# Attention's projection pieces in halves over two steps, with a new order of GpSimd's queue, in a fused attention and feed-forward kernel

## The chip, the cores and the metric

The kernel runs on one core of a Trainium2 chip. A core has TensorE (matmuls, which read SBUF and write PSUM), VectorE (called DVE in the profile), ScalarE (ACT), GpSimd (POOL), and DMA queues that SyncE (SP) issues. Each engine works through its own instructions in order and waits on semaphores for the others. The metric is the device time of one execution in microseconds (us); lower is better. Before the change it is 2101.75 us, the median of 3 runs (2101.75 to 2103.98).

## The reference

Two sandwiched layers over x of 8 batches, each 512 rows by 512 columns, in float32:

```python
x = x + _layernorm(_L0_attn_ref(_layernorm(x, axis=-1), ...), axis=-1)
x = x + _layernorm(_L0_ffn_ref(_layernorm(x, axis=-1), ...), axis=-1)
```

Attention has 16 heads of 32 columns. The head is all rotary (32 of 32), so key and query are the rotated ones:

```python
c_kv = x @ W_dkv + b_dkv                       # 512 -> 128
v = (c_kv @ W_uv + b_uv)                       # 128 -> 512
c_q = x @ W_dq + b_dq                          # 512 -> 128
q_rot = _apply_rotary(c_q @ W_qr + b_qr)       # 128 -> 512
k_rot = _apply_rotary(x @ W_kr + b_kr)         # 512 -> 512
attn = softmax(q @ k.T / sqrt(32))             # per head
out = (attn @ v) @ W_o + b_o
```

`_apply_rotary(t)` is t * cos + swap(t) * sin, where swap exchanges the halves of each head. The feed-forward part transforms its input by a Walsh-Hadamard matrix, multiplies with W_up and W_gate (512 -> 2048), takes silu(gate) * up, transforms again and multiplies with W_down. Both transforms are orthogonal and linear, and the kernel applies the second one to W_down instead of the activations; it calls this folding.

## The kernel before

Attention runs first, all eight batches one after the other, then the feed-forward part, which the change does not touch. In the profiled execution attention's steps run from about 48 us to 894 us, after a start-up in which batch 0's first projections are made.

**Steps.** The scores of a batch are worked out as 4 groups of 4 heads (`NK`), and a group as 4 blocks of 128 keys (`NT`), so a batch is 16 steps and attention 128. Step i of batch b is written b.i here; its place in the group is c = i mod 4, and n counts the groups. The loop `for t in range(NG * NT)` issues one step, and every engine's queue is the order in which this loop writes its instructions: the region is scheduled by hand.

TensorE gets these groups of matmuls in each step, in this order:

1. `scores_t`: the transposed scores t of this key block, for four heads in two PSUM buffers of two banks each. Bfloat16 rows with minus the row maximum come first (the bias rows, L564), then key times query (L573). ACT takes the exponential of each half into p (L585).
2. `weigh`: the previous step's p times the values, into one bank for the whole group (ops, L606).
3. In c = 3, `bias_rows` (L550): the next group's row maxima are transposed into rows. In c = 2, `sums` (L623): the softmax denominators of the group before.
4. `row_max`: the untransposed scores s of the step that comes `AHEAD` = 6 steps later (L527). DVE takes the maximum over each row (L535, two instructions a step). `split` cuts the maxima of a whole group into three bfloat16 parts on GpSimd (L543 to L545); it is issued in c = 1.
5. A piece: a part of the next batch's projections, of the previous batch's output projection, or of the folding.

**Pieces.** They are `key` (L439, four matmuls of 512 columns), `query` (L454, one), `value` (L466, one), `compress` (L407, four, for `ckv` and `cq`), `out_proj` (L661 and L662), `x_flip` (L394, transposes of the normalized x), and `fold` (L485, one matmul; after it four levels of additions on DVE, L493 and L494, one a step, kept in the list `levels`). Which piece stands in which step is in the tables `BETWEEN` (put before s) and `BEHIND` (put last), with `FIRST_` versions for batch 0; the steps in `TWO` have their `BETWEEN` piece just ahead of the `BEHIND` one. A piece "behind" writes the single PSUM bank of `ps_f`, which the sums and the transposed bias rows use too. Where a step has two pieces, the first is wide (here called "beside") and takes a buffer of `ps_s`, the ring of three two-bank buffers in which s and t live (`bank`, L388).

**Rotations.** `rotate` lets ACT copy a key or query piece from PSUM to SBUF (`lin`) and puts the rest, a closure, in the list `turns`: a shuffle on DVE (L420) and three GpSimd operations (L421 to L423). `turn` empties that list; it is called twice a step, once directly behind the exponentials and once behind the row maxima. So a piece of one step is rotated at the start of the next.

**Other work on DVE, GpSimd and ACT.** In c = 1 and 3 GpSimd adds the p of neighbouring key blocks (`add_up`, L594, four operations of 128x512); in c = 0 of the next group DVE adds the two sums (`add_pairs`, L599). DVE also inverts and divides (L644, L657) and makes the statistics of the normalizations (L99, L100); GpSimd works out the inverse standard deviations (L104, L105) and adds the residual (L694). ACT copies the pieces out of PSUM and normalizes x (`x_norm`). `load_x`, `x_stats`, `x_shift`, `x_norm` and `x_flip` bring in the x of two batches later; `early` and `later` set their steps. `fold_load` reads a slice of W_down for a fold, at the steps in `READ`; the folds stand at the steps in `FOLDS`.

In the last batch there is no next batch to project. There, `in_step` puts the first feed-forward inputs through their transposes and Hadamard matmuls (L195, L207), at the places in `ENTRY`, and the last keys, queries and values of batch 7 (key 3, query 3, values 2 and 3) stand in its steps 0 to 3, as in every batch.

Of the kernel before, what the change touches and what calls it, by code (L numbers as in the profile page):

```python
# [10 lines left out]
F32 = mybir.dt.float32  # L11
# [22 lines left out]
def sandwich_kernel(  # L34
# [207 lines left out]
    with ExitStack() as actx:  # L242
# [25 lines left out]
        def load_row(b, t):  # L268

            if b < NB - 1:  # L270
                xr[b, t] = row.tile([P, D], F32, tag="xr", name=f"xr_{b}_{t}", bufs=2)
            else:
                xr[b, t] = fo.tile(
                    [P, D], F32, tag="wwza"[t], name=f"xr_{b}_{t}", bufs=2 - t // 2
                )
            nc.sync.dma_start(out=xr[b, t], in_=x[b, ts(t, P), :])
# [137 lines left out]
        def rotate(dst, ps, bias, scale, name, first=None, second=None):  # L414
            lin = rp.tile([P, S], F32, tag="lin", name=f"lin_{name}")
            nc.scalar.activation(lin, ps, AF.Identity, bias=bias, scale=scale)

            def rest():
                rot = rp.tile([P, S], F32, tag="rot", name=f"rot_{name}", bufs=2)
                nc.vector.stream_shuffle(rot, lin, swap)  # L420
                (first or nc.gpsimd).tensor_mul(lin, lin, cs[:, 0, :])  # L421
                (second or nc.gpsimd).tensor_mul(rot, rot, cs[:, 1, :])
                (first or nc.gpsimd).tensor_add(dst, lin, rot)  # L423

            turns.append(rest)
# [3 lines left out]
        def turn():  # L429

            while turns:
                turns.pop(0)()

# [48 lines left out]
        def fold(n, wide=False):  # L482
            _, w = folds.pop(0)
            ps = bank(wide, f"fd_{n}").rearrange("p (c m) -> p c m", c=NI)
            nc.tensor.matmul(ps, lhsT=h128, rhs=w, start=True, stop=True)  # L485
            z = fo.tile([P, NI, NF], F32, tag="z", name=f"fz_{n}")
            a = fo.tile([P, NI, NF], F32, tag="a", name=f"fa_{n}")
            nc.scalar.copy(z, ps)
# [22 lines left out]
        levels = []  # L511

# [247 lines left out]
        for t in range(3):  # L760
# [13 lines left out]
        BETWEEN = {  # L774
            0: (x_flip, 1, 1), 1: (x_flip, 1, 2), 4: (x_flip, 1, 3),
            8: (query, 1, 0), 9: (query, 1, 1), 12: (query, 1, 2), 13: (x_flip, 2, 0),
        }
        BEHIND = {
            0: (value, 0, 2), 1: (key, 0, 3), 2: (query, 0, 3), 3: (value, 0, 3),
            5: (compress, 1, "cq"), 6: (key, 1, 0), 7: (out_proj, -1, 0),  # L780
            8: (out_proj, -1, 1), 9: (out_proj, -1, 2), 10: (out_proj, -1, 3),
            11: (key, 1, 1), 12: (compress, 1, "ckv"), 13: (value, 1, 0), 14: (key, 1, 2),
            15: (value, 1, 1),
        }

        FIRST_BETWEEN = {i: p for i, p in BETWEEN.items() if i not in (8, 9)}
        FIRST_BEHIND = {
            **BEHIND, 7: (query, 1, 0), 8: (None, NB, None), 9: (key, 1, 1),
            10: (None, NB, None), 11: (query, 1, 1),
        }  # L790
# [5 lines left out]
        FOLDS = [4, 10, 15] + [NK * NT * b + i for b in range(1, NB - 1) for i in (4, 10)]  # L796
        FOLDS.append(NK * NT * (NB - 1) + 1)
        READ = [0] + [g - 3 for g in FOLDS[1:]]


        TWO = (8, 9, 10, 12, 15)

        def piece(table, b, i, wide=False):
            if b == 0 and table is BEHIND and i == 8:
                out_bias()
            pieces = table if b else FIRST_BETWEEN if table is BETWEEN else FIRST_BEHIND
            if i in pieces:
                fn, d, what = pieces[i]
                if 0 <= b + d < NB:
                    fn(b + d, what, *([True] if wide else []))  # L810
            at = NK * NT * b + i
            if at in FOLDS and (table is BETWEEN) == (b > 0 and i in TWO or i == 15 or b == NB - 1):
                fold(FOLDS.index(at), wide)
            if b == NB - 1 and (i, table is BEHIND) in ENTRY:
                in_step(*ENTRY[i, table is BEHIND], 2 * NT)
# [18 lines left out]
        def early(b, i):  # L834

            if b > 0 and i - 3 in OUT:
                residual(b - 1, OUT[i - 3])
            if b + 2 < NB and i in (12, 14, 15):
                x_norm(b + 2, max(i - 13, 0))
            if i == 0 and 0 < b + 1 < NB:  # L840
                x_norm(b + 1, 3)

        def later(b, i):
# [7 lines left out]
            if b + 2 < NB:  # L851
                if i == 4:
                    load_x(b + 2, NT)
                elif 6 <= i < 10:
                    x_stats(b + 2, i - 6)
                elif i == 11:
                    x_shift(b + 2)

        for t in range(NG * NT):
# [8 lines left out]
            turn()  # L868
# [5 lines left out]
            if last_steps:  # L874
                piece(BETWEEN, b, i)
# [12 lines left out]
            if not last_steps and (i not in TWO or b == NB - 1):  # L888
                piece(BETWEEN, b, i)
# [8 lines left out]
            turn()  # L898
# [5 lines left out]
            if levels and (c > 0 or 0 < i and b < 1):  # L904
                levels.pop(0)()
            if small:
# [20 lines left out]
            if i in TWO and b < NB - 1:  # L927
                piece(BETWEEN, b, i, True)
            piece(BEHIND, b, i)
# [685 lines left out]
```

## Time and profile before

| | before |
|---|---|
| median of 3 runs | 2101.75 us |
| the profiled execution's own time | 2102.66 us |
| its span, first to last instruction | 2100.9 us |
| granted TensorE clock, mean | 0.999 |
| TensorE busy with matmuls | 2076.8 us, 99% of the span, 9035 instructions |
| TensorE weight loads | 1057.4 us, 50% |
| GpSimd | 1575.4 us, 75% |
| DVE | 1414.4 us, 67% |
| ACT | 745.3 us, 35% |
| DMA | 218.12 MB, 104 GB/s over the span |

The profile is one execution, so sums are made against its 2102.66 us and not against the median. A matmul counts as busy from when TensorE takes it up until its modelled end, which includes time in which it waits inside the engine; a busy share of 99% therefore does not say that no time is lost. A row of the timeline has the start in us, the duration, the engine, the line of the kernel, and the operation with its output and inputs and their shapes; "x4" means that the row stands for four instructions. A remark in square brackets is the wait ahead of it and what ended it.

### The profile page before, as it was taken

To read this page: it belongs to the slowest core of one execution; us is meant where nothing else is said; L and a number is where in the kernel's file an instruction comes from. 1 tells how busy PE (TensorE), PEld (TensorE's weight loads), DVE (VectorE), ACT (ScalarE), POOL (GpSimd) and SP (SyncE) were. 2 spreads that over 40 slices of the span, in tenths; PEclk is the share of its full clock that TensorE was granted. 3 is DMA by queue.
4 is the path that set the end of the run, shared out by engine and by line. 5 is a ranking of instruction groups with operands and counts; after the bars stand their busy time and mean duration, and the time that the engine had idled before them with its cause. 6 is when DMAs were issued, how large, how long until landed. Compare 5 with 4: busy or idle time off the path is not lost.

```text
span 2100.9 us, 26741 instructions
## 1 busy us (share of the span) xinstructions
PE 2076.8 (99%) x9035; PEld 1057.4 (50%) x9042; DVE 1414.4 (67%) x2356; ACT 745.3 (35%) x1199; POOL 1575.4 (75%) x1629
## 2 busy tenths in 40 slices
PE   8999999999999999999999999999999999999998
PEld 4333333333333333344444677676676766777753
DVE  5698777676767677465545866678866678656542
ACT  3554545555555545522121122222222222222211
POOL 4787979787878889645453678788888879787852
PEclk9999999999999999999999999999999999999999
DMA  3112121212121122237454444444343344444432
GB/s 122 37 31 51 42 54 49 47 51 52 46 57 46 32 66 72 70 104 221 145 166 152 146 143 148 133 138 149 130 157 131 131 137 144 138 158 136 138 112 70
DMA packets 215913, 218.12 MB, mean 104 GB/s; under 512 B 87376, under 2 KB 147920, under 8 KB 215776
## 3 DMA queue, kind: packets, MB, share of 16 engines
q1 hardware_dynamic: 215424, 215.32, 33.2%
q8 instruction: 72, 1.18, 0.2%
q0 software_dynamic: 352, 1.08, 0.1%
q14 instruction: 65, 0.53, 0.1%
HBM read 169.18 MB, written 46.92 MB: 103 GB/s over the span
## 4 chain that ended last, share of the span: by engine, by line
PE 94%; DVE 3%; issue 1%; POOL 1%; ACT 1%; DMA 0%; SPq 0%; POOLq 0%; DVEq 0%; ACTq 0%
PE d L1123 24%; PE psy L1225 18%; PE s L527 6%; PE ops L606 6%; PE ps_k L439 5%; PE ps_y L662 5%; PE t L573 5%; PE u L1106 5%; PE g L1106 4%; PE psz L1516 3%; PE t L564 3%; PE l L623 2%; PE ps_q L454 2%; PE ps_v L466 1%; PE ps_cq L407 1%; PE fxh L207 1%
## 5 line engine op out<-in xcount | busy, mean ns | idle before, releaser
L1225 PE MATMUL psy<-wd,g 128*128 128x512 f32 x896 | 448.9, 592 | 0.0
L535 DVE TENSOR_REDUCE nm<-s 128x2 f32<-128x1024 f32 x256 | 300.8, 1216 | 175.1 <-PE s L527 175.1
L1347 POOL TENSOR_TENSOR pr<-pr,pr 128x512 f32<-128x512 f32 x294 | 391.6, 1357 | 9.0
L594 POOL TENSOR_TENSOR p<-p,p 128x512 f32<-128x512 f32 x244 | 330.2, 1384 | 22.1 <-PE ops L606 22.1
L585 ACT ACTIVATE p<-t 128x1024 f32<-128x1024 f32 x256 | 251.8, 1023 | 89.0 <-PE t L573 89.0
L1123 PE MATMUL d<-xb,wq 128*128 128x256 f32 x992 | 254.2, 380 | 1.9 <-DVE inner L1139 1.4
L1123 PEld LDWEIGHTS d<-tt,wq 128*128 128x128 f32 x864 | 164.0, 190 | 144.4 <-issue 106.0
L1123 PE MATMUL d<-tt,wq 128*128 128x256 f32 x864 | 233.8, 379 | 0.2 <-DVE pr L1144 0.2
L1140 POOL TENSOR_TENSOR pr<-inner 128x256 f32<-128x256 f32 x168 | 126.0, 750 | 138.5 <-DVE inner L1139 105.9
L1123 PEld LDWEIGHTS d<-xb,wq 128*128 128x128 f32 x992 | 186.7, 190 | 62.4 <-issue 30.1
L1225 PEld LDWEIGHTS psy<-wd,g 128*128 128x128 f32 x896 | 169.7, 190 | 49.3 <-issue 29.4
L1136 ACT COPY inner<-d 128x256 f32<-128x256 f32 x168 | 62.6, 373 | 309.6 <-PE d L1123 291.5
L1132 ACT COPY inner<-d 128x256 f32<-128x256 f32 x168 | 62.6, 372 | 300.3 <-PE d L1123 193.2
L527 PE MATMUL s<-kT,qT 32*128 32x512 f32 x1024 | 153.8, 639 | 0.7 <-DVE nm L535 0.7
L573 PE MATMUL t<-qT,kT 32*128 32x512 f32 x1024 | 142.8, 598 | 0.0
L606 PE MATMUL ops<-p,v 128*32 128x512 f32 x1024 | 136.8, 605 | 0.0
L1142 POOL TENSOR_TENSOR pr<-pr,inner 128x256 f32<-128x256 f32 x168 | 136.5, 813 | 0.0
L1123 PE MATMUL d<-T,wq 128*128 128x256 f32 x496 | 127.6, 380 | 0.2
L1144 DVE TENSOR_TENSOR pr<-d,inner 128x256 f32<-128x256 f32 x168 | 70.5, 420 | 75.5 <-PE d L1123 72.9
L439 PE MATMUL ps_k<-xT,wkr_sb 128*128 128x512 f32 x256 | 118.3, 605 | 0.7 <-ACT xT L397 0.7
L662 PE MATMUL ps_y<-wo_sb,oT 128*128 128x512 f32 x256 | 115.8, 593 | 0.9 <-DVE oT L657 0.6
L1135 DVE TENSOR_TENSOR inner<-d,inner 128x256 f32<-128x256 f32 x168 | 70.5, 419 | 62.4 <-PE d L1123 62.0
(219 smaller groups left out, 3263.8 us busy)
## 6 DMA issues: line engine op xcount, KB each, us to landing
wq<-wdeep SPq DMA_DIRECT2D x168, 448.0 KB, 4.2
wd<-wdd SPq DMA_DIRECT2D x112, 256.0 KB, 2.8
wdeep<-w SPq DMA_DIRECT2D x32, 448.0 KB, 5.5
xr<-in_x SPq DMA_DIRECT2D x32, 256.0 KB, 2.8
xin<-x1d SPq DMA_DIRECT2D x32, 256.0 KB, 4.0
xres<-x1d SPq DMA_DIRECT2D x32, 256.0 KB, 3.3
out<-fy SPq DMA_DIRECT2D x32, 256.0 KB, 2.0
rec<-rd SPq DMA_DIRECT2D x124, 64.0 KB, 2.0
```

The lines of the kernel that those rows point to most:

```text
L439: nc.tensor.matmul(ps, lhsT=wkr_sb[:, k, ts(g, P)], rhs=xT[b][:, k, :], start=(k == 0), stop=(k == NK - 1),)
L527: nc.tensor.matmul(sp[j // 2][:, j % 2, :], lhsT=qT[b][rows, g, ts(qc, P)], rhs=kT[b][rows, g, :], start=True, stop=True,)
L535: nc.vector.tensor_reduce(nms[n][:, qc, 2 * h : 2 * h + 2], sp[h], AX.X, ALU.max, negate=True)
L573: nc.tensor.matmul(sp[j // 2][:, j % 2, :], lhsT=kT[b][rows, g, ts(c, P)], rhs=qT[b][rows, g, :], start=False, stop=True,)
L585: nc.scalar.activation(pt[n, c, h], sp[h], AF.Exp)
L594: nc.gpsimd.tensor_add(into, into, pt[n, c, j // 2][:, j % 2, :])
L606: nc.tensor.matmul(o_ps[n][j * DH : (j + 1) * DH, :], lhsT=vv[b][:, c, ds(g * P + j * DH, DH)], rhs=pt[n, c, j // 2][:, j % 2, :], start=( ...
L662: nc.tensor.matmul(ps, lhsT=oT[b][:, k, ts(qc, P)], rhs=wo_sb[:, k, :], start=False, stop=(k == NK - 1),)
L1106: nc.tensor.matmul(ps, lhsT=w[:, SLOT[n], k, :], rhs=rhs[:, k, :], start=k == 0, stop=k == 1)
L1123: nc.tensor.matmul(ps, lhsT=w[:, INNER[m]], rhs=rhs[m], start=True, stop=True)
L1225: nc.tensor.matmul(ys_[t], lhsT=g[:, ts(t, P)], rhs=w, start=n == 0, stop=n == NI - 1)
L1347: nc.gpsimd.tensor_add(pr[n][:, h], pr[a][:, h], pr[b][:, h])
```

## The change

It touches attention's steps alone.

**Pieces in halves.** `both(b, i, small, large)` puts a small piece (a query, a value or a fold) together with a large one (a key or a compress) over steps i and i + 1. Each step makes half the columns of both (256 of 512), the small piece in one half of the `ps_f` bank and the large one in the other half, and two ACT copies take them out. There are 40 such pairs; a step of a pair has all its matmuls of these pieces at 256 columns. The tables are replaced by `put`, which writes a dictionary `plan` from step and place ("between", "beside", "behind") to work.

**A new layout of the batch.** In batches 1 to 6 pairs stand at steps 1, 3, 5, 11, 13 and 15 (the last reaching into the next step 0); the four values stand beside the output projections in steps 7 to 10; x is flipped between, in steps 9, 12, 13 and the next step 0, for two batches later. Key 3 and query 3 are made with the others in the batch before. In batch 6 the pair at 13 is taken apart: key 3 of batch 7 is made in 6.14, and query 3 in 7.2, while values 2 and 3 of batch 7 are made in batch 6. Two folds stand in batch 7, at 7.3 and at 7.8. Batch 6's step 15 and batch 7's steps 0 and 1 have no piece behind; of the first feed-forward input, step 7.0 has the transposes, as before.

**Rotations.** `turn(True)` runs one rotation at a time. The first place, ahead of `weigh`, is used in c = 0 and 2 and in step 13 alone; the second, behind the row maxima, in c = 0, 1 and 3 except in step 13. In c = 1 and 3 GpSimd's block sums, and in c = 1 the split too, so come before the rotation in its queue; in step 13 the rotation still comes first.

**Rest.** x is loaded at step 14 of three batches earlier, its statistics made at steps 1, 2, 3 and 5, its shift at step 7 and its norms at 8, 11, 12 and 14 (all moved). Fold levels run in c = 0 in batch 7 alone (before: in batch 0 alone), and one of the small operations of `small` (batch 0's output bias) waits while a level runs. The last batch's residual rows use the fold's buffers in another order.

The core of the diff:

```diff
             lin = rp.tile([P, S], F32, tag="lin", name=f"lin_{name}")
             nc.scalar.activation(lin, ps, AF.Identity, bias=bias, scale=scale)
+            rotation(dst, lin, name, first, second)
+        def rotation(dst, lin, name, first=None, second=None):
...
             while turns:
                 turns.pop(0)()
+                if one:
+                    return
         def key(b, g, wide=False):
             if g == 0:
...
+            n, w = folds.pop(0)
             ps = bank(wide, f"fd_{n}").rearrange("p (c m) -> p c m", c=NI)
             nc.tensor.matmul(ps, lhsT=h128, rhs=w, start=True, stop=True)
             z = fo.tile([P, NI, NF], F32, tag="z", name=f"fz_{n}")
+            nc.scalar.copy(z, ps)
+            fold_levels(n, w, z)
+        def fold_levels(n, w, z):
             a = fo.tile([P, NI, NF], F32, tag="a", name=f"fa_{n}")
...
             def level(src, dst, h):
                 sv = src.rearrange("p (a t b) n -> p a t (b n)", t=2, b=h)
...
             )
         levels = []
...
+        HC = S // 2
+        split_in_two = {}
+        def half(h, ps, fn, b, what):
+            cols = ts(h, HC)
...
+                if h == 0:
+                    split_in_two["z"] = fo.tile([P, NI, NF], F32, tag="z", name=f"fz_{n}")
+                z = split_in_two["z"]
+                blocks = ts(h, NI // 2)
+                pv_ = ps.rearrange("p (c m) -> p c m", m=NF)
+                nc.tensor.matmul(pv_, lhsT=h128, rhs=w[:, blocks, :], start=True, stop=True)
+                def leave():
+                    nc.scalar.copy(z[:, blocks, :], pv_)
+                    if h == 1:
+                        folds.pop(0)
+                        fold_levels(n, w, z)
+                return leave
+            if fn is value:
+                if what == h == 0:
...
+                if what == h == 0:
+                    qT[b] = qkv.tile([P, NK, S], F32, tag="qT", name=f"qT_{b}")
+                if h == 0:
+                    split_in_two["q"] = rp.tile([P, S], F32, tag="lin", name=f"lin_q{b}_{what}")
+                dst = split_in_two["q"]
+                nc.tensor.matmul(
+                    ps, lhsT=wqr_sb[:, ts(what, P)], rhs=cT[b, "cq"][:, cols], start=True, stop=True
+                )
+                def leave():
+                    nc.scalar.activation(
+                        dst[:, cols], ps, AF.Identity, bias=bqs[:, what : what + 1], scale=QSCALE
+                    )
+                    if h == 1:
+                        rotation(qT[b][:, what, :], dst, f"q{b}_{what}")
...
-        BETWEEN = {
-            0: (x_flip, 1, 1), 1: (x_flip, 1, 2), 4: (x_flip, 1, 3),
-            8: (query, 1, 0), 9: (query, 1, 1), 12: (query, 1, 2), 13: (x_flip, 2, 0),
-        }
-        BEHIND = {
-            0: (value, 0, 2), 1: (key, 0, 3), 2: (query, 0, 3), 3: (value, 0, 3),
-            5: (compress, 1, "cq"), 6: (key, 1, 0), 7: (out_proj, -1, 0),
-            8: (out_proj, -1, 1), 9: (out_proj, -1, 2), 10: (out_proj, -1, 3),
-            11: (key, 1, 1), 12: (compress, 1, "ckv"), 13: (value, 1, 0), 14: (key, 1, 2),
-            15: (value, 1, 1),
-        }
...
+        plan = {}
+        def put(b, i, place, *work):
+            if len(work) == 1 or work[1] < NB:
+                plan.setdefault((NK * NT * b + i, place), []).append(work)
+        def both(b, i, small_, large):
+            large = large if large[1] < NB else None
+            small_ = small_ if len(small_) == 1 or small_[1] < NB else None
+            if large and small_:
+                for h in range(2):
+                    put(b, i + h, "behind", halves, 0, h, small_, large)
+            elif small_:
+                put(b, i, "behind", *small_)
+        def halves(_, h, small_, large):
+            ps = bank(False, f"ps_{large[0].__name__}_{large[1]}_{large[2]}_{h}")
+            both_ = [(*small_, None, None)[:3], large]
+            for leave in [half(h, ps[:, ts(n, HC)], *which) for n, which in enumerate(both_)]:
+                leave()
+        both(0, 0, (value, 0, 2), (key, 0, 3))
+        put(0, 2, "behind", query, 0, 3)
+        put(0, 3, "behind", value, 0, 3)
+        both(0, 4, (fold,), (compress, 1, "cq"))
+        both(0, 6, (query, 1, 0), (key, 1, 0))
+        put(0, 8, "behind", out_bias)
+        both(0, 9, (query, 1, 1), (key, 1, 1))
+        put(0, 11, "beside", query, 1, 2)
+        put(0, 11, "behind", compress, 1, "ckv")
+        both(0, 12, (value, 1, 0), (key, 1, 2))
+        put(0, 14, "beside", query, 1, 3)
+        put(0, 14, "behind", key, 1, 3)
+        for t in range(3):
+            put(0, 15 + t, "beside", value, 1, t + 1)
+        both(0, 15, (fold,), (compress, 2, "cq"))
+        for t, i in enumerate((0, 1, 4)):
+            put(0, i, "between", x_flip, 1, t + 1)
+        for b in range(NB):
+            for t, i in enumerate((9, 12, 13, 16)):
+                put(b, i, "between", x_flip, b + 2, t)
+        for b in range(1, NB):
+            both(b, 1, (query, b + 1, 0), (key, b + 1, 0))
+            both(b, 3, (query, b + 1, 1), (compress, b + 1, "ckv"))
+            if b < NB - 1:
+                both(b, 5, (fold,), (key, b + 1, 1))
+            for t in range(NT):
+                put(b, 7 + t, "beside", value, b + 1, t)
+                put(b, 7 + t, "behind", out_proj, b - 1, t)
+            both(b, 11, (query, b + 1, 2), (key, b + 1, 2))
+            if b == NB - 2:
+                put(b, 13, "behind", fold)
+                put(b, 14, "behind", key, NB - 1, 3)
+                put(b, 18, "behind", query, NB - 1, 3)
+                continue
+            both(b, 13, (query, b + 1, 3), (key, b + 1, 3))
+            if b < NB - 1:
+                both(b, 15, (fold,), (compress, b + 2, "cq"))
+        put(NB - 1, 3, "behind", fold)
+        put(NB - 1, 8, "beside", fold)
...
+        READ = [1]
+        for b in range(NB - 1):
+            READ += [NK * NT * b + 10 + 2 * (b < NB - 2), NK * NT * (b + 1) + 2]
+        READ[-1] = NK * NT * (NB - 1)
+        READ.append(NK * NT * (NB - 1) + 4)
+        def piece(place, b, i):
+            for fn, *which in plan.get((NK * NT * b + i, place), ()):
+                fn(*which, *([True] if place == "beside" else []))
+            entry = i, {"between": False, "behind": True}.get(place)
+            if b == NB - 1 and entry in ENTRY:
+                in_step(*ENTRY[entry], 2 * NT)
...
-            if b + 2 < NB and i in (12, 14, 15):
-                x_norm(b + 2, max(i - 13, 0))
-            if i == 0 and 0 < b + 1 < NB:
-                x_norm(b + 1, 3)
+            if b + 2 < NB and i in NORMS:
+                x_norm(b + 2, NORMS.index(i))
+            if b == i == 0:
+                x_norm(1, 3)
...
             ends_group = c == NT - 1 and n + 1 < NG
             if not ends_group:
                 second()
-            turn()
+            if c in (0, 2) or i == 13:
+                turn(True)
             if c == 0 and n > 1:
...
-            if not last_steps and (i not in TWO or b == NB - 1):
-                piece(BETWEEN, b, i)
+            if not last_steps:
+                piece("between", b, i)
...
                 if u % NT == NT - 1:
                     split(u // NT)
             early(b, i)
-            turn()
+            if c != 2 and i != 13:
...
-            if levels and (c > 0 or 0 < i and b < 1):
+            busy_dve = False
+            if levels and (c > 0 or b == NB - 1):
+                busy_dve = len(levels) % 5 != 1
                 levels.pop(0)()
-            if small:
+            if small and not busy_dve:
                 small.pop(0)()
             if t in READ:
                 fold_load(READ.index(t))
...
-            if i in TWO and b < NB - 1:
-                piece(BETWEEN, b, i, True)
-            piece(BEHIND, b, i)
+            piece("beside", b, i)
+            piece("behind", b, i)
```

## The prediction

> **What bounds the kernel now.** I read the page's slices, then its chain of waits, then TensorE's timeline through attention. [...]
>
> ```profile
> PE   8999999999999999999999999999999999999998
> ...
> POOL 4787979787878889645453678788888879787852
> ...
> PE 94%; DVE 3%; issue 1%; POOL 1%; ACT 1%; DMA 0%; SPq 0%; POOLq 0%; DVEq 0%; ACTq 0%
> ```
>
> TensorE is busy in every slice and is 94% of the chain, so time can come only from gaps between its instructions. They hide in stretched rows; I take the distance from one group's start to the next one's. Attention's 128 steps run from 48 to 894 us; two of them:
>
> ```profile
> 270.52 0.40 PE L564 MATMUL t<-brow,ones_b 32*128 32x512 bf16 x4
> 270.74 1.03 PE L573 MATMUL t<-qT,kT 32*128 32x512 f32 x8
> 271.70 1.07 PE L606 MATMUL ops<-p,v 128*32 128x512 f32 x8
> ...
> 273.56 1.14 PE L527 MATMUL s<-kT,qT 32*128 32x512 f32 x8
> 274.63 1.13 PE L454 MATMUL ps_q<-cq,wqr_sb 128*128 128x512 f32 x2
> 275.69 0.71 PE L564 MATMUL t<-brow,ones_b 32*128 32x512 bf16 x4
> 276.02 1.24 PE L573 MATMUL t<-qT,kT 32*128 32x512 f32 x8
> 277.19 1.06 PE L606 MATMUL ops<-p,v 128*32 128x512 f32 x8
> ```
>
> From bias to ops is 1.18 us in the first and 1.50 in the second, which follows a piece of only 1.06: there half of the bias rows wait for a PSUM buffer that DVE's first row maximum (1.2 each) still holds. So a short piece costs the next step 0.32. Adding all such excesses over each group's usual distance gives about 30 us: 7.4 in batch 0, 2.7 in each of batches 2 to 5, a little less in 1 and 6, some 7 in batch 7. That is all there is to win. The batches last 100.9, 108.6, four times 108.7, 108.1 and 93.5.
>
> **A step of the new plan.** Bias 0.23, t 0.96, ops 1.00, s 1.07: 3.26. Every fourth step adds sums (0.86), another one bias transposes (0.33); a flip is 0.59. A whole key piece is 3.63, a small one 1.06.
>
> **Halving: +1.5.** 40 pairs are cut; in each, 10 matmul records of 512 columns become 20 of 256. The FFN's timeline has both widths:
>
> ```profile
> 1303.25 1.02 PE L1225 MATMUL psy<-wd,g 128*128 128x512 f32 x2
> 1304.11 1.03 PE L1123 MATMUL d<-tt,wq 128*128 128x256 f32 x4
> 1304.97 0.59 PE L1225 MATMUL psy<-wd,g 128*128 128x512 f32 x1
> ```
>
> Four of 256 take 0.86, two of 512 take 0.86: a pair costs 20 x 0.216 - 10 x 0.428 = 0.04 more. [...] The row shows this very form, weights loaded for each record, at half; I take the row (0 to 3). The number of changes between tiled and full matmuls stays. The halves' ACT copies (0.37 each for 128x256 on the page, two 0.8, against 0.69 whole) end before the exponentials at 1.3 into the step.
>
> **Short steps filled: -10.9.** Every middle step now ends with 2.36 (halves of a pair) or more, and DVE's first maximum is out 1.3 after s. 34 waits of 0.32 in batches 1 to 6 go. What is late next is s, for an exponential: 0.2 in four steps a batch (5, 8, 9, 12; now 1, 4, 5, 8), which stays; batch 6, without flips, gets three more, **+0.6**.
>
> **Values beside out_proj: +4.8.** They move to steps 7 to 10. A "beside" piece takes the fifth buffer in a ring of three, that of the second t, so it waits for the second exponential, which comes late in a step with bias transposes. 0.15 shows it:
>
> ```profile
> 145.31 1.14 PE L527 MATMUL s<-kT,qT 32*128 32x512 f32 x8
> 146.98 1.12 PE L485 MATMUL fd<-fw,h 128*128 128x512 f32 x2 [0.53 <-ACT p L585]
> ```
>
> 0.6 each in step 7 of six batches and in 0.11 and 0.15 (4 to 5 in all). Behind it waits out_proj, hence all of TensorE.
>
> **Rotations behind the splits: +5.0.** From step 13 to the next step 1 GpSimd's queue is now: q2, block sums, split, residual, k2, sums, q3, k3, sums, split. Rotations 4 x 3.84, sums 3 x 4.9, splits 2 x 1.5, residual 1.25: 34.3, each from an undisturbed stretch of its timeline. Beside it DVE adds tensors in SBUF, and the two collide. The pair sums alone, then against GpSimd:
>
> ```profile
> 422.58 2.35 DVE L599 TENSOR_TENSOR p<-p,p 128x1024 f32<-128x1024 f32 x2
> ...
> 454.97 4.20 DVE L599 TENSOR_TENSOR p<-p,p 128x1024 f32<-128x1024 f32 x2
> ...
> 455.96 2.13 POOL L423 TENSOR_TENSOR kT<-lin_k,rot_k 128x512 f32<-128x512 f32 x1
> 458.05 2.26 POOL L694 TENSOR_TENSOR y<-xr,y 128x512 f32<-128x512 f32 x1
> ```
>
> Both lose 1.9. [...] The rows give 1.9, 0.4 and 0.2 each, 2.7, which I take. The queue starts 3.2 into step 13, behind DVE's pair sums and shuffle, and ends 40.2 after that step's start. TensorE wants the second split's rows after 6.2+6.5+5.9+6.2+5.8+6.5 = 37.1, plus 2.2 into step 3: 39.3. Late by 0.9 to 1.0, in step 3 of batches 2 to 6; s and all TensorE stand behind. Bounds: on time (0)[...]. Step 13's exception keeps q2 early: its buffer is needed by the third key's copy, which ACT would reach 0.4 before the rotation ends; ACT's exponential just misses the delay.
>
> **DVE: +1.2 (0 to 4).** With GpSimd busy from step 15 to 6, a fold level costs DVE about 2 instead of 0.8 (L494 is seen at 0.42 and 1.48), pair sums 4.2. DVE then runs up to 2 us behind, its first maximum 0.1 to 0.4 ahead of t: I take 0.2 a batch.
>
> **Batch 0: -5.4.** 6 us of work come in (two flips, key, query, half a compress, less folds) and leave batches 6 and 7; over all batches this is nil. Of 7.4 stall about 2 stay: DVE, 23.9 and 23.3 busy of 25 from 100 to 150 us, loses 1.5 folds, and the bias's small steps avoid fold levels. Bounds -3 and -6.
>
> **Batch 7: +7.5.** It loses 4.7 us of work, but 6.15, 7.0 and 7.1 are left without any piece, and t waits for DVE there. 6.15 makes 7.0's bias wait 1.3. In 7.0 DVE has shuffle, level, xflat and statistics ahead of its maxima, then pair sums and a level ahead of 7.1's. With these at their undisturbed times 7.0 to 7.2 stall 5.1; at their contended times 9.7; now it is 1.8. So 3.3 to 8; GpSimd's queue (k2, sums, k3, sums) runs through, so near the upper. A second fold in step 8 is work, counted above.
>
> **At nothing.** Norms, statistics and loads of x move within a batch: ACT is 35% busy, statistics keep their number, and SP now issues x's 1 MB load at step 14, three steps before its first use (now two), waiting there for the last norm; behind it SP has only loads due later. No TensorE wait now ends with a DMA. Fold reads stay about three steps ahead. If a load were late, DVE's statistics would hold up the maxima: a few us once a batch. FFN is untouched.
>
> **Sum.** 1.5 - 10.9 + 0.6 + 4.8 + 5.0 + 1.2 - 5.4 + 7.5 = +4.3. The profiled execution took 2102.66 (span 2100.9), so 2107.0; the median shown is 0.9 less: **2106.1**.
>
> **Rivals.**
> *Not slower:* GpSimd's queue is in time. The split at step 3 decides: if the queue ends 1.0 earlier (DVE's sums meeting its pauses), the 5.0 fall away, DVE keeps its slack (-1.2) and 7.0 to 7.2 pay 5.1 (-4): 2096. For it: 1 in 40 is within my reading. Against: there is no pause between step 13 and 2. 0.3.
> *GpSimd decides:* the split comes 2.5 late and ACT's half copy waits for a rotation: +8, so 2114. For it: nothing has slack; against: a batch has 91 us of GpSimd work in 108. 0.2.
> *The stalls stay:* the change doesn't even out the steps, DVE being late everywhere: half of the 10.9 is lost, 2111.5. 0.07. [...] The forecast 0.42.
>
> A measurement tells about 0.2% (4.2 us) from no change: faster is below 2097.5, slower above 2106. Faster 0.24 (the first rival's better part), same 0.27, slower 0.49. Eight in ten: 2094 to 2115.
>
> **What would show it.** Halves at 0.216 a record. No bias rows of 0.7 in steps 0 to 5. The value of step 7 waiting 0.5 for ACT. Bias transposes of step 3 waiting for GpSimd in batches 2 to 6. 7.0 to 7.2 near 22 us (19.8 now). A steady batch near 108.7. I am wrong if that is under 107.5 or over 110, or if 7.0 to 7.2 stay under 18.

## The result and the profile after

| | before | after |
|---|---|---|
| median | 2102.14 us (4 runs, 2101.75 to 2103.98) | 2113.88 us (4 runs, 2112.07 to 2114.44) |
| profiled execution, its span | 2102.66, 2100.9 | 2114.37, 2112.6 |
| granted TensorE clock, mean | 0.999 | 0.996 |

The ratio is 1.0055, with a 95% interval from 1.0043 to 1.0067: the change made the kernel slower, by more than the 0.2% that a measurement can tell. The forecast was 2106.1, in the right direction and 7.8 us short; the measured time lies in its range.

The page of the changed kernel, its slices and its chain of waits:

```profile
PE   8999999999999998999999999999999999999998
...
POOL 4798696969696978745444578888888879787862
...
PE 88%; POOL 5%; DVE 5%; issue 1%; ACT 1%; DMA 0%; SPq 0%; POOLq 0%; DVEq 0%; ACTq 0%
```

TensorE has lost 6% of the chain, and GpSimd and DVE have gained as much. The one slice of 8 within TensorE's row is the sixteenth of 52.8 us each, 792 to 845 us: the end of batch 6 and the start of batch 7. By batches, from the first bias rows of one to those of the next:

| | before | after | difference |
|---|---|---|---|
| start-up, to step 0.0 | 46.78 | 45.85 | -0.9 |
| batch 0 | 102.11 | 104.74 | +2.6 |
| batch 1 | 108.62 | 113.53 | +4.9 |
| batches 2 to 5, each | 108.67 | 109.14 to 109.20 | +0.5 |
| batch 6 | 108.09 | 106.93 | -1.2 |
| steps 7.0 to 7.2 | 19.8 | 22.6 | +2.8 |
| steps 7.3 to 7.14 | 70.4 | 72.3 | +1.8 |

(The prediction counts from the second half of batch 0's first bias rows, 1.2 us later; hence its 100.9 for batch 0.)

Rows from a steady batch on TensorE's timeline, to be read against the two steps shown for before:

```profile
492.12 0.70 PE L558 MATMUL ps_key<-cq,wqr_sb 128*128 128x256 f32 x2
492.66 1.89 PE L584 MATMUL ps_key<-xT,wkr_sb 128*128 128x256 f32 x8
494.48 0.39 PE L646 MATMUL t<-brow,ones_b 32*128 32x512 bf16 x4
...
500.95 0.40 PE L646 MATMUL t<-brow,ones_b 32*128 32x512 bf16 x4
501.17 1.03 PE L655 MATMUL t<-qT,kT 32*128 32x512 f32 x8
502.13 1.06 PE L688 MATMUL ops<-p,v 128*32 128x512 f32 x8
504.25 0.40 PE L632 MATMUL ps_b<-ident_b,parts 128*128 128x128 bf16 x4 [1.05 <-POOL parts L627]
...
519.67 0.76 PE L646 MATMUL t<-brow,ones_b 32*128 32x512 bf16 x4
...
530.68 1.12 PE L471 MATMUL ps_v<-wuv_sb,ckv 128*128 128x512 f32 x2 [0.53 <-ACT p L667]
```

Half a pair takes 2.36 from its first row to the next bias rows (492.12 to 494.48), and those last 0.39 and not 0.71: the short steps are filled. One stretched row is left, in step 4.6 (0.76 at 519.67), where the first row maximum comes late behind DVE's pair sums (3.97). The price stands in the brackets: in step 4.3 the bias transposes wait 1.05 for GpSimd's split, and in 4.7 the value waits 0.53 for an exponential.

What stands out is batch 1. TensorE's timeline of its step 1.6, then DVE's ahead of it:

```profile
188.85 0.39 PE L646 MATMUL t<-brow,ones_b 32*128 32x512 bf16 x2
190.91 0.39 PE L646 MATMUL t<-brow,ones_b 32*128 32x512 bf16 x2 [1.67 <-DVE nm L617]
190.91 1.24 PE L655 MATMUL t<-qT,kT 32*128 32x512 f32 x8
192.09 1.66 PE L688 MATMUL ops<-p,v 128*32 128x512 f32 x8
193.50 1.95 PE L705 MATMUL l<-p,ones_f 128*32 128x512 f32 x8
```

```profile
181.88 2.27 DVE L617 TENSOR_REDUCE nm<-s 128x2 f32<-128x1024 f32 x2
184.09 3.96 DVE L681 TENSOR_TENSOR p<-p,p 128x1024 f32<-128x1024 f32 x2
187.97 1.75 DVE L365 TENSOR_TENSOR bo_in<-bo_in,bo_hi 128x512 f32<-128x512 f32 x1
189.64 2.34 DVE L617 TENSOR_REDUCE nm<-s 128x2 f32<-128x1024 f32 x2
```

The second half of the bias rows waits for a row maximum that DVE begins at 189.64; s was there at 186.5. Ahead of it stand the pair sums and L365, a small operation of the output bias. That belongs to batch 0: the changed loop skips `small` in a step with a fold level. Then something else shows: ops takes 1.66 and the sums 1.95, where 1.06 and 1.04 are usual. Windows of 3.41 us, as long as the clock was low, show it as the number behind the five engines' busy times; the first of these is TensorE's:

```profile
189.01:192.43 3.42, 1.75 (x16) 0.57 (x17) 3.42 (x5) 1.03 (x3) 3.42 (x4) 1.00 0.01 2
192.43:195.84 3.41, 3.41 (x20) 0.90 (x16) 1.66 (x5) 1.86 (x3) 3.12 (x7) 0.50 0.00 0
```

After the wait TensorE was granted half its clock for 3.41 us. The same is seen in batch 7, where the wait is longer:

```profile
818.04 0.39 PE L646 MATMUL t<-brow,ones_b 32*128 32x512 bf16 x2
823.12 0.61 PE L646 MATMUL t<-brow,ones_b 32*128 32x512 bf16 x2 [4.69 <-DVE nm L617]
823.12 2.31 PE L655 MATMUL t<-qT,kT 32*128 32x512 f32 x8
825.36 1.94 PE L688 MATMUL ops<-p,v 128*32 128x512 f32 x8
```

DVE's timeline ahead of it:

```profile
815.78 4.42 DVE L681 TENSOR_TENSOR p<-p,p 128x1024 f32<-128x1024 f32 x2
820.12 1.48 DVE L501 TENSOR_TENSOR fa<-fz 128x256 f32<-128x256 f32 x1
821.52 0.41 DVE L502 TENSOR_TENSOR fa<-fz 128x256 f32<-128x256 f32 x1
821.85 2.34 DVE L617 TENSOR_REDUCE nm<-s 128x2 f32<-128x1024 f32 x2
```

The row maxima stand behind the pair sums and a fold level. t has 1.24 behind a wait for DVE elsewhere, and 2.31 here; the clock was 0.50 from 820.48 to 827.30. So my theory after the result: the layout costs about what was predicted in the steady batches; the rest comes from two places where DVE is late (1.6, by the bias's operations; 7.2, by pair sums and fold levels), and the clock adds to both. The rivals: the pair sums alone make 1.6 late; the long rows are late operands and not the clock; the order of rotations or the halves themselves are the loss.

### The profile page after: what moved, and what is told of

Same layout as the page of the kernel before. It is cut to its first block, busy times and chain, and to the rows that moved or that the text cites. A ratio compares the mean times of both kernels' runs of the same rounds, so it can differ in the third digit from the quotient of the medians.

```text
span 2112.6 us, 27655 instructions
## 1 busy us (share of the span) xinstructions
PE 2072.7 (98%) x9442; PEld 1131.1 (54%) x9442; DVE 1409.4 (67%) x2356; ACT 757.2 (36%) x1279; POOL 1567.5 (74%) x1629
## 4 chain that ended last, share of the span: by engine, by line
PE 88%; POOL 5%; DVE 5%; issue 1%; ACT 1%; DMA 0%; SPq 0%; POOLq 0%; DVEq 0%; ACTq 0%
PE d L1250 23%; PE psy L1352 18%; PE s L609 5%; PE ps_y L744 5%; PE ops L688 5%; PE u L1233 5%; PE g L1233 4%; PE t L655 4%; PE ps_key L584 3%; PE psz L1643 3%; POOL p L676 2%; PE t L646 2%; PE ps_v L471 2%; PE l L705 1%; PE fxh L207 1%
## 5 line engine op out<-in xcount | busy, mean ns | idle before, releaser
L676 POOL TENSOR_TENSOR p<-p,p 128x512 f32<-128x512 f32 x244 | 311.6, 1308 | 45.5 <-PE ops L688 28.7
L655 PE MATMUL t<-qT,kT 32*128 32x512 f32 x1024 | 137.4, 595 | 0.0
L744 PE MATMUL ps_y<-wo_sb,oT 128*128 128x512 f32 x256 | 115.8, 593 | 0.6 <-DVE oT L739 0.6
L1262 DVE TENSOR_TENSOR inner<-d,inner 128x256 f32<-128x256 f32 x168 | 70.4, 419 | 62.4 <-PE d L1250 61.9
L1287 DVE SCALAR_TENSOR_TENSOR g<-pr,wsu 128x512 f32<-128x512 f32 x96 | 109.3, 1140 | 3.2 <-POOL pr L1474 3.2
```

The lines of the kernel that those rows point to most:

```text
L655: nc.tensor.matmul(sp[j // 2][:, j % 2, :], lhsT=kT[b][rows, g, ts(c, P)], rhs=qT[b][rows, g, :], start=False, stop=True,)
L676: nc.gpsimd.tensor_add(into, into, pt[n, c, j // 2][:, j % 2, :])
L744: nc.tensor.matmul(ps, lhsT=oT[b][:, k, ts(qc, P)], rhs=wo_sb[:, k, :], start=False, stop=(k == NK - 1),)
```

## The experiments

All are edits of the changed kernel, and each ran once, but for the last, which ran 20 times. Effects below 2 us are read from the steps of the trace: the time of one run also depends on the granted clock, and its mean differs between runs of one kernel (0.996 to 0.998 in the four of the changed one, which took 2114.44 to 2112.07).

**The bias's operations, one a step again.**

```diff
-            if small and not busy_dve:
+            if small:
```

> The changed kernel, with the output bias's small DVE operations issued one a step again, fold level or not. Theory: the 4 us by which batch 1 is longer than a steady batch plus its two extra values come from these operations slipping into steps 1.1 and 1.5, where GpSimd's rotations and DVE's pair sums collide; with them back in batch 0, step 1.6 loses its wait of 1.8 us and the rows at half clock behind it: batch 1 from 113.5 to 109.2 - 110.3 us, the whole 3 to 4 us less (2110 to 2111). Rival: the pair sums and fold levels alone make DVE late at 1.6: batch 1 stays above 112.5, and batch 0 gets longer by as much as it gains.

Measured: batch 1 took 110.46 (-3.07), batch 0 0.27 more. Step 1.6 on TensorE's timeline:

```profile
190.86 0.77 PE L646 MATMUL t<-brow,ones_b 32*128 32x512 bf16 x4
192.42 1.06 PE L688 MATMUL ops<-p,v 128*32 128x512 f32 x8
193.30 1.04 PE L705 MATMUL l<-p,ones_f 128*32 128x512 f32 x8
```

The wait and the slow rows are gone, so the skipped operations made them. The time as a whole was missed: 2114.1. The 3 us came back elsewhere as clock: between 20 and 40 us, where the kernel is the same, the windows show 0.96 and 0.87 where the changed kernel had 1.00, and step 0.0 begins 1.5 later; steps 7.0 to 7.2 took 0.9 more (0.50 to 0.79 from 812 to 828).

**The last residual on DVE.**

```diff
-            nc.gpsimd.tensor_add(y, xr[b, qc], y)
+            (nc.vector if qc == NT - 1 else nc.gpsimd).tensor_add(y, xr[b, qc], y)
```

> The changed kernel, with the residual addition of each batch's last 128 rows on DVE instead of GpSimd (1.27 us out of GpSimd's queue at step 15). Theory: the bias transposes of step 3 in batches 2 to 6 wait because GpSimd's queue from step 13 on has no pause and ends 1.07 late; 1.27 less in it ends the wait: each of the batches 2 to 5 from 109.15 to about 108.1, the whole 4 to 5.5 less (2109 to 2110). Rival: the queue restarts at each wait for ACT and DVE (a rotation waits for its shuffle), so a shorter queue only waits elsewhere: the wait of step 3 stays over 0.7.

Measured: a steady batch of 108.55 (-0.6), 2106.98. The bias transposes of step 4.3 on TensorE, and GpSimd's block sums in step 3.14:

```profile
500.37 0.40 PE L632 MATMUL ps_b<-ident_b,parts 128*128 128x128 bf16 x4 [0.41 <-POOL parts L627]
```

```profile
467.61 5.43 POOL L676 TENSOR_TENSOR p<-p,p 128x512 f32<-128x512 f32 x4
```

GpSimd's queue is the cause: a shorter one shortens the wait. But of 1.27 taken out only 0.6 arrive. The four sums of 3.14 take 5.43 instead of 4.95; the first of them begins beside the residual on DVE (1.40 there). The split behind them loses another 0.16. From there to the late split of step 3 the queue takes the same time in both kernels (25.4 and 25.5). The rest of this run's gain is not the edit's alone: step 1.6 has its wait (1.66) but no slow rows behind it (ops 1.07; -1.65), and steps 7.0 to 7.2 are 2.9 shorter, with the clock low for a shorter time (0.74 and 0.83 over 808 to 816; in the changed kernel 0.50 for 6.82).

**TensorE kept busy in 7.0 and 7.1.**

```diff
+            if b == NB - 1 and i < 2:
+                idle = bank(False, f"idle_{i}")
+                for _ in range((8, 30)[i]):
+                    nc.tensor.matmul(idle[:, 0:P], lhsT=wsdp_bc[:, 0:P], rhs=wsdp_bc[:, P : 2 * P], ...)
```

> The changed kernel, with 8 matmuls of 128 columns behind step 7.0 and 30 behind 7.1, into a free PSUM bank and read by nothing. They add no result and take no wait away: DVE's row maxima, which t waits for in 7.1 and 7.2, stay where they are. Theory: the rows of t, ops and sums in 7.2 last twice as long because TensorE's granted clock fell to 0.5 after its idle time; with TensorE kept busy the clock stays at 1.0, and steps 7.0 to 7.2 last 19.2 to 20.2 us instead of 22.6 (the whole 2.4 to 3.4 less, 2111 to 2112). Rival: the rows are long because their operands come late (values, keys, exponentials): 22.6 stays, or grows.

Measured: the clock stayed at 1.00, and 7.0 to 7.2 took 22.7. That looks like the rival, but step 7.2 had no wait left at all: the 30 matmuls behind 7.1 took 6.96 us and outlasted DVE by 2.1. The same with 20:

> The changed kernel, with 8 matmuls of 128 columns behind step 7.0 and 20 (instead of 30) behind 7.1, read by nothing. 30 of them took 6.96 us at full clock and outlasted the wait by 2.1; 20 at 0.232 take 4.64 and end with DVE's last row maximum. Theory: of step 7.2's excess the granted clock of 0.5 makes 2.1 us, the wait for DVE the rest: 7.0 to 7.2 last 20.4 to 20.8 us instead of 22.6. Rival: the clock changes nothing, and t, ops and sums of 7.2 stay long: 22.4 or more.

Measured: 20.6, with the clock at 1.00. TensorE's timeline of 7.2 (the profile shows each of the 20 float32 matmuls as two):

```profile
817.07 4.73 PE L1060 MATMUL idle<-wsdp_bc 128*128 128x128 f32 x40
821.74 0.49 PE L646 MATMUL t<-brow,ones_b 32*128 32x512 bf16 x4
821.96 1.13 PE L655 MATMUL t<-qT,kT 32*128 32x512 f32 x8
823.02 1.07 PE L688 MATMUL ops<-p,v 128*32 128x512 f32 x8
```

Work that nobody needs, put into a wait, makes the kernel 2.0 us faster there: that is the clock's share in 7.2. The useless matmuls end when DVE's first maximum does (821.75), so the 20.6 that are left are work and waiting for DVE. That pair sums and fold levels make DVE late here was read from its rows; no run takes them away. In 1.6, where nothing was changed, this run shows the other half of the proof: the same wait (1.69), and no slow rows behind it (ops 1.06; -1.62 against the changed kernel), as in three more of the runs reported here (the last residual on DVE, the values, the last key: waits of 1.66 to 1.67, ops of 1.06 to 1.07).

**The values away from step 7.**

```diff
-                put(b, 7 + t, "beside", value, b + 1, t)
+                put(b, (6, 8, 9, 10)[t], "beside", value, b + 1, t)
```

> The changed kernel, with the values of batches 1 to 6 beside steps 6, 8, 9 and 10 instead of 7 to 10. Theory: the value of step 7 waits 0.60 for the second exponential, which comes late in a step with bias transposes; in step 6 (c = 2) the exponential is out in time, as in step 10, and the wait goes: 0.5 to 0.6 less in each of six batches, 3 to 3.6 in all (2110.5 to 2111.4). Rival: the wait is for the ring's order and moves with the value, or step 6, which already holds half a pair and the sums, stalls on DVE's maxima: no gain (2113.5 to 2115).

Measured: step 7 -1.55, step 6 +0.87, a steady batch of 108.45 (-0.7). The time was 2108.02, 2.5 below what was expected, 1.7 of it the clock in step 1.6 (1.00 from 192 to 196, in the changed kernel 0.57). Step 4.6:

```profile
519.08 1.14 PE L609 MATMUL s<-kT,qT 32*128 32x512 f32 x8
520.15 1.13 PE L471 MATMUL ps_v<-wuv_sb,ckv 128*128 128x512 f32 x2
```

The value follows s with no wait, so it was the place and not the ring.

**The pairs uncut.**

```diff
-                for h in range(2):
-                    put(b, i + h, "behind", halves, 0, h, small_, large)
+                put(b, i, "behind", *small_)
+                put(b, i + 1, "behind", *large)
```

> The changed kernel with its pairs uncut: the small piece whole in the first step, the large one whole in the second. Theory: halving costs 0.04 us a pair on TensorE and spares the 0.32 us by which the step behind a short piece waits for DVE's row maximum; uncut, a steady batch has six such steps and takes 109.15 + 6 x 0.28 = 110.8 us (110.3 to 111.3), the whole 2121 to 2125. Rival: half-width matmuls with a weight load each cost more than their share, so that uncut pieces take less: 109.2 or less.

Measured: a steady batch of 110.04, 2120.47. The step behind a short piece:

```profile
460.39 1.12 PE L459 MATMUL ps_q<-cq,wqr_sb 128*128 128x512 f32 x2
461.44 0.71 PE L646 MATMUL t<-brow,ones_b 32*128 32x512 bf16 x4
```

The stretched rows are back (0.71), and the batch is longer, by 0.9 and not by 1.7: step 3 no longer waits for GpSimd, which gives back 1.07. GpSimd's rows at step 4.3, which begins at 506.98, show why:

```profile
506.42 0.26 POOL L627 CAST parts<-nm 128x16 bf16<-128x16 f32 x1
506.57 1.49 POOL L424 TENSOR_TENSOR lin_q<-lin_q,cs 128x512 f32<-128x512 f32 x1
```

Here the split is out before the step begins; in the changed kernel it came 3.2 us into it. Uncut, a query is whole a step earlier and its rotation is done earlier, so that from step 13 on three rotations and not four stand ahead of this split. So halving fills the short steps as it should, about 2 us a batch, but in this layout the late split of step 3 comes with it, and what is left is 0.9.

**The rotations first.**

```diff
-            if c in (0, 2) or i == 13:
-                turn(True)
+            turn()
...
-            if c != 2 and i != 13:
-                turn(True)
+            turn()
```

> The changed kernel with the rotations as before: all that are ready, directly behind the exponentials, ahead of block sums and split. Theory: GpSimd has the same work between step 13 and step 1, so step 3 stays late by about 1; at step 13 both rotations (7.7 us) now stand ahead of sums and split, so that step 15's bias transposes wait some 2.5 us too, and step 7's and 11's perhaps: a steady batch takes 110 to 113 us instead of 109.15, the whole 2118 to 2135. Rival: the order of GpSimd's queue was no help, or put the wait of step 3 there in the first place: a steady batch of 108.1 to 109.2.

Measured: a steady batch of 115.8 to 119.5, 2157.5. The mechanism was the expected one, but a batch lost 6.6 to 10.3 us and not 1 to 4, most of it in step 15 (4.6 to 6.0). Step 15, on TensorE and on GpSimd:

```profile
612.48 0.40 PE L632 MATMUL ps_b<-ident_b,parts 128*128 128x128 bf16 x4 [2.89 <-POOL parts L627]
...
614.64 3.35 PE L584 MATMUL ps_compress_cq<-xT,wdq_sb 128*128 128x256 f32 x8
```

```profile
597.92 1.28 POOL L424 TENSOR_TENSOR lin_q<-lin_q,cs 128x512 f32<-128x512 f32 x1 [3.18 <-DVE rot_q L423]
...
605.56 4.96 POOL L676 TENSOR_TENSOR p<-p,p 128x512 f32<-128x512 f32 x4
610.45 0.73 POOL L625 CAST parts<-nm 128x16 bf16<-128x16 f32 x1
```

Two rotations, 7.6 us, stand ahead of the sums, and the first waits for its shuffle. The transposes wait 2.89, and then the compress takes 3.35 where eight such matmuls take 1.89: this wait too was followed by slow rows (mean clock of the run 0.988). That part of 1.5 us was in no expectation.

**No exception in step 13.**

```diff
-            if c in (0, 2) or i == 13:
+            if c in (0, 2):
...
-            if c != 2 and i != 13:
+            if c != 2:
```

> The changed kernel without step 13's exception: there too the rotation stands behind block sums and split. Theory (the prediction's claim on this exception): the buffer of the third query is then free only after 4.9 us of sums, 1.5 of split and 3.8 of rotation, 4 to 5 us into step 14; ACT's copy of the next key half waits for it, and the exponentials of step 14 stand behind that copy, so TensorE waits 3 to 5 us in each of the batches 1 to 5: a steady batch of 112 to 114 us, the whole 2129 to 2140. Rival: GpSimd's queue starts 1.5 to 2 us earlier, since it no longer waits for a shuffle in step 13, the wait of 1.07 in step 3 goes, and the copy waits for little: a steady batch of 108.1 to 109.0.

Measured: a steady batch of 116.1 to 116.4, 2146.89. ACT's and TensorE's rows of step 14:

```profile
490.40 0.48 ACT L589 ACTIVATE lin_k<-ps_key,pv 128x256 f32<-128x256 f32 x1 [7.00 <-POOL qT L426]
```

```profile
490.93 1.93 PE L705 MATMUL l<-p,ones_f 128*32 128x512 f32 x8 [5.86 <-ACT lin_k L589]
```

The copy waits for the third query's rotation, as the prediction said of this exception, but for longer than the 3 to 5 us expected. Step 14 is 7.6 to 8.2 longer, of which the clock is a part (the sums take 1.93, elsewhere 1.04; mean clock of the run 0.99); step 3's wait is gone (-1.07), but that does not matter against this.

**Batch 7's last key in 7.1.**

```diff
-                put(b, 14, "behind", key, NB - 1, 3)
+                put(b, 17, "behind", key, NB - 1, 3)
```

> The changed kernel, with batch 7's last key made in step 7.1 (as before the change) instead of 6.14. Theory: in 7.1 it fills 3.6 us in which TensorE waits for DVE, and its rotation leaves GpSimd's queue when DVE's pair sums collide with it, so that DVE is 1.5 to 2 us earlier and the clock doesn't fall: batch 6 with steps 7.0 to 7.2 takes 121 to 125 us instead of 129.5, the whole 4.5 to 8.5 less. Rival: DVE's own work (pair sums, fold levels, inputs of the feed-forward part) makes the wait, and 6.14 and 6.15 without the key wait as long as it took: 127 or more.

Measured: batch 6 106.78, 7.0 to 7.2 20.5, together 127.3: more like the rival. 6.14 lost 3.74 and 6.15 gained 3.55. But DVE's work fills only a part of 6.15 (1.11 in the first of these rows):

```profile
800.37 0.39 PE L646 MATMUL t<-brow,ones_b 32*128 32x512 bf16 x2 [1.11 <-DVE nm L617]
...
804.62 0.40 PE L632 MATMUL ps_b<-ident_b,parts 128*128 128x128 bf16 x4 [2.00 <-POOL parts L627]
```

The longer part, 2.00, is the split, which stands behind the third query's rotation in GpSimd's queue. Step 13's exception is there for a copy that batch 6 does not have. This gave the next kernel.

**Together.** The edits on the bias's operations, the residual, the values and the last key, and the exception left out in batch 6 alone:

```diff
+            if c in (0, 2) or i == 13 and b != NB - 2:
...
+            if c != 2 and (i != 13 or b == NB - 2):
```

> The changed kernel with four edits of these experiments (small operations each step, values beside 6, 8, 9 and 10, the last residual of a batch on DVE, batch 7's last key in 7.1), and in batch 6 no exception in step 13, since no key half is copied there. Expected by adding the edits' own effects: a steady batch of 107.9; batch 1 of 109 to 110; in 6.15 the wait of 3.5 us that the moved key uncovered (split behind the third query's rotation) goes. Together 2096 to 2102. Rival: in 6.13 to 7.2 DVE's own work of some 28 us sets the length whatever GpSimd does: 2101 to 2105.

Measured: 2097.35, a steady batch of 107.86, batch 1 109.76, batch 6 102.74, and 7.0 to 7.2 19.3. Step 6.15 is 2.1 shorter than with the key alone moved: about the wait for the split.

> As the one before, and the last two values of batch 7 are made behind 6.15 and 7.0 instead of beside 6.9 and 6.10. Theory: steps 6.13 to 7.2 are bound by DVE, so 1.9 us of TensorE's work put there cost nothing and are saved in 6.9 and 6.10: 1.5 to 2 us less than the kernel before it in this list, 2094 to 2100. Rival: the waits of those steps have gone with the other edits, and the work only moves: no difference over 0.5.

Measured: 2097.73 (20 runs, 2097.06 to 2099.5) against 2101.83 of the kernel before the change: a ratio of 0.998 (0.9973 to 0.9987): 4 us faster than that kernel, and 16 us faster than the changed one. Between the two, attention from its first step on is 1.8 us shorter in the second, as expected; the time does not show it, since this run's start-up was 1.25 longer than that one's. The waits in front of 7.0 and 7.1, and its chain:

```profile
794.91 0.39 PE L646 MATMUL t<-brow,ones_b 32*128 32x512 bf16 x2 [0.73 <-DVE nm L617]
...
800.47 0.39 PE L646 MATMUL t<-brow,ones_b 32*128 32x512 bf16 x2 [0.28 <-DVE nm L617]
```

```profile
PE 95%; DVE 3%; ACT 1%; issue 1%; DMA 0%; POOL 0%; SPq 0%; POOLq 0%; DVEq 0%; ACTq 0%
```

## Why the prediction came out as it did

The direction was right, and most steps held to a few tenths:

- *Halving.* Two steps of halves take 2 x 2.36 = 4.72, as was worked out from the row of the feed-forward part; whole pieces 4.69.
- *Short steps filled.* No bias row of steps 0 to 5 is over 0.5 in the steady batches, and uncutting the pairs brings the rows of 0.7 back. Step 6, which the prediction did not name, has one of 0.76.
- *Values.* 0.53 of wait was shown in the row of step 0.15, 0.53 came in step 7 of six batches, and moving the value away took it back.
- *Rotations behind splits.* The split was to be 0.9 to 1.0 late in step 3 of batches 2 to 6; it is 1.06 to 1.12 late. That a queue of 40 us was summed to a tenth was luck in part. It rested on taking DVE's collisions from rows: 1.9 for the pair sums, 0.4 for a division, 0.2 for each of two fold levels. And the term was booked to the order of the rotations alone; the uncut pairs, with the same order, have no such wait, so the halves have a part in it.
- *Step 13's exception.* The reason given was right. "Just misses" was not: without it ACT waits 7.00.
- *Batch 7.* 22 us were forecast for 7.0 to 7.2, 22.6 came. The reason was half right and the number luck: with DVE's waits alone it would have been 20.6, and the slow clock, which no term contained, added 2.0.

The step that failed is **"Batch 0: -5.4"**, with the clause that the bias's small steps avoid fold levels. I booked this line of the diff as a relief for batch 0's DVE. It postpones: an operation waits wherever a level runs, so that batch 1 gets three of them (in steps 1.1, 1.5 and 1.7) where it had one, and the one of 1.5 takes 1.75 against GpSimd, between the pair sums and the maxima. Batch 1 was costed like any other: 0.24 for halves, -1.9 for six filled steps, 0.6 for the value, 0.2 for DVE, together -0.9. It has +4.9, of which 1.9 are two values that batch 7 no longer makes: 3.9 more than its terms, 3.3 of it in step 1.6, half by the wait and half by the slow clock behind it; with the operations back in batch 0, these 3.3 go. The start-up and batch 0 together grew by 1.7 instead of 0.6.

The other term that was missing is the **granted clock**. TensorE's longest wait in attention was 1.27 before, and the clock of that trace is 1.00 through all of it; the forecast added waits of 2 and 5 us and priced them at their length. Measured, 1.6 cost 1.65 more by this and 7.2 2.0. The clock was 0.50 for 3.41 us in 1.6 and for twice that around 7.2. In the 3.41 us ahead of the fall in 1.6 TensorE was busy for 1.75, about half. In two runs half clock followed this wait; in four others no slow rows did. One of the four:

```profile
188.73:192.14 3.41, 1.75 (x16) 0.57 (x17) 3.41 (x5) 1.03 (x3) 3.41 (x4) 1.00 0.01 2
192.14:195.55 3.41, 3.41 (x28) 1.43 (x21) 2.38 (x6) 2.07 (x3) 3.12 (x7) 1.00 0.00 0
```

These are the windows of step 1.6 in the run with the last residual on DVE, with a wait of 1.66; the clock stays at 1.00.

Of the 7.4 us between the sum and the measurement, batch 1 has 3.9 and start-up with batch 0 has 1.1. Each of the batches 2 to 5 grew by 0.48 where the terms make 0.14, 1.4 in all; there, steps 5 and 6 wait 0.45 for DVE instead of the 0.2 taken, which is 1.0 of the 1.4. Steps 7.0 to 7.2 have 0.6, and 0.4 is left, of which I can't say where it is.

The rival "GpSimd decides" gave 2114, almost the measured time, for a reason that did not occur: step 3 was never 2.5 late.

## What to carry to other kernels

When an edit lets work wait for a better moment, find the moment in which it now runs and cost it there; deferred work lands where the queue is fuller. Look at the granted clock before a wait on TensorE is costed at its length: here the wait of 4.69 ahead of 7.2 was followed by half clock, and that of some 1.67 in 1.6 in two executions of six, 2.0 and 1.65 us on top. Where such a wait can't be removed, matmuls that nobody needs gave that back here, as long as they ended in time (2.0 with 20 of them behind 7.1, nothing with 30). And where two engines have work for most of a period, a hand-written order is worth keeping only for the batches whose conflict it solves: the exception in step 13 was worth about 7 us in each of five batches, and in the sixth it held the split back by 2.0 once the key that hid it was moved.

## What the runs showed of the hardware

- TensorE's granted clock fell twice in attention of the changed kernel's trace, to 0.50: for 3.41 us in step 1.6 (192.43 to 195.84) and for 6.82 around 7.2 (820.48 to 827.30). In the 3.41 us ahead of each fall TensorE was busy for 1.75 and 1.37. In the first 3.41 of the second it was busy for 0.77, and the clock stayed at 0.50; in the last 3.41 of each it was busy throughout, and the clock was 1.00 behind them.
- A longer wait was cheaper than a short one. In the changed kernel no slow row follows the wait of 2.21 ahead of 7.1 (812.6 to 814.8; ops 1.06): the clock was 1.00 in both stretches of 3.41 us that this wait lies in (from 810.24 and from 813.65), with TensorE busy for 2.34 and 2.28. The wait of 1.67 in step 1.6 was followed by half clock in two executions out of six, which moved the time of otherwise equal steps by 1.65.
- Taking work from GpSimd to DVE moved only half of it: 1.27 out of one queue shortened the wait behind it by 0.6 (1.05 to 0.41), and most of the rest shows in the four GpSimd sums that began beside the moved one (5.43 instead of 4.95) and the split behind them (0.16).
- Float32 matmuls of 256 columns, with a weight load each, took half of those of 512: 0.216 and 0.428 from row to row before the change, and in the changed kernel eight of 256 took 1.82, with the change to the tiled bias rows behind them.
